# A perceiver's cross-attention: a context block's projection in one piece instead of two

## The chip, the cores and the metric

The kernel runs on one core of a Trainium2 chip. The metric is the device time of one execution in microseconds (us); the time given for a kernel is the median of several runs. One execution was recorded by the hardware profiler, and all rows of the profile come from it. Engines: PE (TensorE: matrix products; PEld is its weight load), DVE (VectorE), ACT (ScalarE), POOL (GpSimd) and SP, which here only issues transfers (DMA).

## The reference

Four layers work on 128 tokens of 256 dims, `x`. Each has a cross-attention over a context of 12544 rows of 192 dims, a self-attention among the 128 tokens, and a mixture of experts. The change is in the cross-attention of layers 0 to 2 (16 heads of 16 dims):

```python
k = (context @ Wk).reshape(B, M, HEADS, hd).transpose(0, 2, 1, 3)
v = (context @ Wv).reshape(B, M, HEADS, hd).transpose(0, 2, 1, 3)
scores = jnp.einsum('bhid,bhjd->bhij', q, k) * scale
scores = jnp.where(context_mask[:, None, None, :], scores, max_neg)
attn = jax.nn.softmax(scores, axis=-1)
out = jnp.einsum('bhij,bhjd->bhid', attn, v)
```

That is layer 0, which alone has a mask. Layers 1 and 2 add biases to the projections, and layer 1 clips the scores and replaces them by a mean where one is not a number (the guard). Layer 3 has another form of attention, with heads of 64 dims.

## The kernel before

All is 32-bit float. The context is cut into 25 blocks of 512 keys (the last has 256). It lies transposed in memory, dims on partitions, and since 192 dims are more than 128 partitions, a block comes as two transfers: `ctxA`, the upper 128 dims of all 512 keys, and `ctxB`, the lower 64 dims, folded so that each half of the block's keys has 64 partitions. Four tiles of each take turns, so SP loads a block as soon as the block four before it has been read (lines 378 to 396).

The 16 heads are done in two halves of 8 (`g` = 0 and 1, line 600), and each half in two passes over the keys, written in `attend_twice_in`. The first pass projects keys and values of all blocks and finds each head's highest score; the second recomputes the scores, lowers them by that maximum, and takes exponentials and the weighted sum. The change is in the first pass.

One projection of a block (`project`, line 152) fills one *pair*, a PSUM tile of two banks with 128 x 2 x 512 numbers: in each bank 256 columns of keys and 256 of values. The dims are summed in two steps. `low=0` multiplies the upper dims: 2 key products of 256 columns and 4 value products of 128, each with all 128 partitions. `low=1` adds the lower dims: as many products with 64 partitions. A 32-bit product runs as two on PE, so the profile counts 12 for either step. After the lower step ACT copies keys and values out of the pair (lines 127 to 136), in layers 1 and 2 with the keys' bias. In layer 1 POOL also adds up the context for the guard (lines 98 and 99), which DVE reduces at lines 931 and 932.

`highest` (line 530) makes scores: a pair again, two products of 32 partitions x 512 keys (line 538; in layer 0 each begins with a product that brings in the mask, line 537, from a row that POOL makes), and one maximum on DVE over 128 x 1024 numbers (line 539, tile `parts`). A block has four of these: two sets of 64 query-and-head combinations (`s` = 0, 1) times two halves of the heads (`half`). That is eight score products a block. The four of one `s` work in four separate groups of 32 rows of the array and run beside each other.

All pairs, for projections and scores alike, come from one pool of four (`self.psum(ppr=4)`, line 501). A new tile takes the buffer that has been free longest in the order of the program, and waits until its last reader is done. PE works in the order in which its products are listed.

What stands between the scores is listed by `steps` (line 138). The first pass has 50 steps, one for each block and `s`; after step `t`'s two maxima come the projections in `steps[t]`. Two blocks are projected before the pass in any case, in layers 1 and 2 eight before its first half (`early`, line 88, beside the layer before). So 23 are left to spread over 46 steps, or 17 in the first halves of layers 1 and 2. The last three blocks get only keys there (`values` is false); their values follow after the pass, while DVE works on the maxima found.

These lines set what is left to do and how fast it is spread:

```python
todo = [(b, low, b < NSB - 3) for b in range(2, NSB) for low in range(2) if g * NSB + b >= self.done]
to = min(n, -(-n * (t + 1) // (2 * NSB - 4)))
while to < n and 2 * todo[to][0] + todo[to][1] <= t + 4:
```

An entry is half a projection, so with 46 entries each step has one: the upper piece after `s` = 0, the lower one after `s` = 1. With 34 entries, two of every three to four steps have one.

Of the kernel before, what the change touches and what calls it, by code (L numbers as in the profile page):

```python
# [28 lines left out]
HB = SB // 2  # L29
NSB = -(-S2 // SB)  # L30
# [14 lines left out]
def bc(ap, axis, n):  # L45

    ap = ap.unsqueeze(axis)
    shape = list(ap.shape)
    shape[axis] = n
    return ap.to_broadcast(shape)  # L50


class Keys:
# [4 lines left out]
    def __init__(self, net, wk, wv, groups, bias=None, sums=None):  # L58
        self.net, self.nc, self.wk, self.wv, self.bias, self.sums = net, net.nc, wk, wv, bias, sums
        self.context = net.context(groups * NSB)  # L60
        self.started, self.done, self.rest = {}, 0, None
        if sums is not None:
            self.nc.gpsimd.memset(sums, 0.0)

# [23 lines left out]
    def early(self, n=EARLY):  # L88

        for b in range(n):  # L90
            for low in range(2):
                self.project(0, b, low)

    def add_up(self, g, b):
        if g == 0 and self.sums is not None:
# [42 lines left out]
    def steps(self, g):  # L138

        todo = [(b, low, b < NSB - 3) for b in range(2, NSB) for low in range(2) if g * NSB + b >= self.done]
        n, at, out = len(todo), 0, []
        for t in range(2 * NSB):
            to = min(n, -(-n * (t + 1) // (2 * NSB - 4)))
            while to < n and 2 * todo[to][0] + todo[to][1] <= t + 4:
                to += 1
            out.append(todo[at:to])
            at = to
        return out  # L150

    def project(self, g, b, low, values=True):


        if g * NSB + b < self.done:
            return
        if not low:
            self.add_up(g, b)
            self.started[g, b] = self.net.early_pair() if self.rest is None else self.net.pair()
        p = self.started[g, b]  # L160
        self.keys_into(p, g, low, [b])
        if values:
            self.values_into(p, g, low, [b], HB)
        if low:
            n = len(self.halves(b))
            self.keep_keys(g, b, p[:, :n, :HB])
            if values:
                self.keep_values(g, b, p[:, :n, HB:])
            self.done = g * NSB + b + 1

    def project_values(self, g, blocks):
        p = self.net.pair()
# [33 lines left out]
class Net:  # L206
# [300 lines left out]
    def attend_twice_in(self, pool, o, qz, keys, masked, clip, between):  # L507
# [11 lines left out]
        def mask_rows(g, b):  # L519

            src = d["mask"].rearrange("c p -> (c p)")[b * SB : min(S2, b * SB + SB)].unsqueeze(0)
            n = src.shape[-1]
            to = rows8[b % 3]
            nc.sync.dma_start(to[0:P:32, :n], src.to_broadcast([4, n]))
            row = pool.tile([P, SB], BF16, tag="row", name="row", bufs=3)
            nc.gpsimd.tensor_scalar(row[:, :n], to[:, :n], 0.0, 1.0, ALU.is_gt, ALU.subtract)
            nc.gpsimd.tensor_scalar(row[:, :n], row[:, :n], self.bar, None, ALU.mult)
            return row

        def highest(g, b, s, half, parts):  # L530

            n = min(SB, S2 - b * SB)
            x = self.pair()
            for i in range(2):
                r = tiles[2 * half + i]
                if masked:
                    nc.tensor.matmul(x[:, i, :n], self.ones16[r, :], rows[-1][r, :n], start=True, stop=False)
                nc.tensor.matmul(x[:, i, :n], qz[r, g, s, :], keys.kT(b)[r, :n], start=not masked, stop=True)  # L538
            nc.vector.tensor_reduce(parts[:, s, 2 * half : 2 * half + 2, b], x[:, :, :n], AX.X, ALU.max)  # L539

        def lowered(parts):


            neg = self.stat(8, "neg8").rearrange("p (s t) -> p s t", s=2)
            nc.vector.tensor_reduce(neg, parts, AX.X, ALU.max, negate=True)
            if clip is not None:
                self.ts(neg, neg, -clip, clip, ALU.max, ALU.min)
            short = self.sp.tile([P, 2, 4], BF16, tag="short", name="short")
            for j in range(2):
                nc.vector.tensor_copy(short, neg)  # L550
                nc.vector.tensor_copy(wide[:, :, :, j], short)
                self.tt(neg, neg, wide[:, :, :, j], ALU.subtract)
            nc.vector.tensor_copy(wide[:, :, :, 2], neg)
            p = self.pair()
            for s in range(2):
                nc.tensor.transpose(p[:, 0, s * P : s * P + P], wide[:, s].rearrange("p t e -> p (t e)"), self.ident)
            m = pool.tile([P, 2, HB], BF16, tag="low", name="low", bufs=1)
            nc.vector.tensor_copy(m, bc(p[:, 0, :HB], 1, 2))  # L558
            return m.rearrange("p c n -> p (c n)")
# [30 lines left out]
        def weighted(g, c, es, acc):  # L590
            v = keys.v(c // 4)
            for j in range(2):
                for s in range(2):
                    for t in range(4):
                        nc.tensor.matmul(  # L595
                            acc[32 * t : 32 * t + 17, s, :P], v[:, c % 4 + j, 2 * t + s, :], es[t // 2][:, t % 2, j, s, :],
                            start=c + j == 0, stop=c + j == S2 // P - 1,
                        )

        for g in range(2):  # L600
            if g == 0:
                for b in range(2):
                    for low in range(2):
                        keys.project(g, b, low)
            parts = pool.tile([P, 2, 4, NSB], F32, tag="parts", name="parts", bufs=1)
            steps = keys.steps(g)
            for b in range(NSB):
                if masked:
                    rows.append(mask_rows(g, b))
                for s in range(2):  # L610
                    for half in range(2):
                        highest(g, b, s, half, parts)
                    for step in steps[2 * b + s]:
                        keys.project(g, *step)
                if between is not None and g == 0 and b == 3:
                    between[0]()

            keys.project_values(g, [NSB - 3, NSB - 2])
            keys.project_values(g, [NSB - 1])
            if between is not None:  # L620
                between[1][g][0](self.pair)
            m = lowered(parts)
            if between is not None:
                between[1][g][1]()
            floor = None
            if clip is not None:
                floor = []
                for half in range(2):
                    x = self.pair()
                    for i in range(2):  # L630
                        r = tiles[2 * half + i]
                        nc.tensor.matmul(x[:, i, :], self.ones16[r, :], m[r, :], start=True, stop=True)
                    floor.append(pool.tile([P, 2, SB], F32, tag=f"floor{half}", name="floor", bufs=1))
                    self.ts(floor[half], x, -clip, None, ALU.add)
            acc = self.pair()
            nc.vector.memset(acc[:, :, :P], 0.0)
            made = []
            for c in range(0, S2 // P, 2):
                made.append((g, c, [weights(g, c, half, m, floor) for half in range(2)], acc))
                if len(made) > (1 if clip is None else 2):  # L640
                    weighted(*made.pop(0))
            if g == 0:
                for b in range(2):
                    for low in range(2):
                        keys.project(1, b, low)
            for step in made:
                weighted(*step)
            oT = pool.tile([P, 2, P], F32, tag="oT", name="oT", bufs=1)
            nc.vector.tensor_copy(oT, acc[:, :, :P])  # L649
            p = self.pair()  # L650
            for s in range(2):
                nc.tensor.transpose(p[:, 0, s * P : s * P + P], oT[:, s, :], self.ident)
            new = p[:, 0, :HB].rearrange("p (s t e) -> p s t e", s=2, t=4)
            r = self.stat(8, "r8").rearrange("p (s t) -> p s t", s=2)
            nc.vector.reciprocal(r.unsqueeze(3), new[:, :, :, 16:17])
            to = o[:, g * P : g * P + P].rearrange("p (t s e) -> p s t e", s=2, e=16)
            for s in range(2):
                self.tt(to[:, s], new[:, s, :, :16], bc(r[:, s], 2, 16), ALU.mult)
# [1082 lines left out]
```

## Time and profile before

| | us |
|---|---|
| median of 4 runs | 3122.86 (3120.72 to 3126.52) |
| the profiled execution | 3123.04 |
| its span, first to last instruction | 3121.2 |
| layer 0, first pass, maxima of both halves | 21.0 to 154.9, 295.2 to 429.9 |
| layer 1, the same | 698.6 to 822.0, 958.8 to 1089.4 |
| layer 2, the same | 1378.6 to 1500.8, 1641.9 to 1772.5 |

The times of the passes are the starts of their first and last maximum. A row of the profile reads: line, engine, operation, output<-inputs, shapes, count, then busy time and mean duration, then the engine's idle time before them and what ended it. In a timeline the first two columns are start and duration of a run of like instructions, and in brackets the idle time before it and its releaser. In the view of one tile, "PE pair L538: 12.0, 11" says that the engine sat idle 12.0 us in 11 stretches until a product of line 538 ended. Times of PE's products overlap, because they are pipelined, so the start of the next group says more than the end of the last.

### The profile page before, as it was taken

Reading aid. Unit: us, or ns where it says so; the run is one execution under the profiler, and the core shown is the slowest. Engines: PE = TensorE matmul, PEld = TensorE weight load, DVE = VectorE, ACT = ScalarE, POOL = GpSimd, SP = SyncE. Lnnn points to the kernel's source line nnn. Section 1 sums busy time; section 2 is a strip of 40 time slices with the busy share of each in tenths; the row PEclk is TensorE's granted clock in tenths of the full one; section 3 lists DMA queues with packets and bytes.
Section 4 is the critical chain, followed back from the end, with each engine's and each line's share of the span. In section 5 each row is a group of like instructions: output and inputs, shape, how many; then the busy total and the mean of one; then the engine's idle time right before and its main releaser. Section 6 shows DMA issues by size and latency. Waiting matters only on the chain.

```text
span 3121.2 us, 78239 instructions
## 1 busy us (share of the span) xinstructions
PE 2971.7 (95%) x35065; PEld 2253.6 (72%) x35065; DVE 1957.4 (63%) x2300; ACT 1470.0 (47%) x1869; POOL 295.3 (9%) x349
## 2 busy tenths in 40 slices
PE   8999999879999999899999999899999999999979
PEld 6677667545576576665676576489889889889858
DVE  7801850439997897769208603467777777777844
ACT  1187139511383185311572285256556555556521
POOL 6601640212000000110000001000000000000000
PEclk9999989989999998999999999899999999999979
DMA  4100210552002102341102105322222222222436
GB/s 134 52 18 26 69 41 3 186 201 60 27 3 62 50 18 70 127 132 51 31 8 72 50 3 198 123 82 84 84 79 88 81 86 81 87 81 85 121 108 204
DMA packets 165254, 246.83 MB, mean 79 GB/s; under 512 B 19853, under 2 KB 106831, under 8 KB 164920
## 3 DMA queue, kind: packets, MB, share of 16 engines
q1 hardware_dynamic: 160200, 227.67, 23.3%
q0 software_dynamic: 4608, 14.16, 1.4%
q8 instruction: 275, 4.51, 0.6%
q14 instruction: 59, 0.48, 0.0%
q10 hardware_dynamic: 112, 0.01, 0.0%
HBM read 241.65 MB, written 0.13 MB: 77 GB/s over the span
## 4 chain that ended last, share of the span: by engine, by line
PE 79%; DVE 11%; ACT 5%; issue 3%; DMA 2%; POOL 0%; SPq 0%; DVEq 0%; ACTq 0%; POOLq 0%
PE pair L102 20%; PE pair L538 9%; PE v L102 8%; PE pair L575 7%; PE pair L595 6%; PE sc L701 6%; PE acc L743 6%; PE ps L275 4%; DVE parts L539 3%; ACT e L581 3%; PE acc L275 2%; PE pair L567 2%; DVE e L289 2%; PE kv L102 2%; PE ps L1532 1%
## 5 line engine op out<-in xcount | busy, mean ns | idle before, releaser
L539 DVE TENSOR_REDUCE parts<-pair 128x2 f32<-128x1024 f32 x600 | 679.3, 1198 | 105.0 <-PE pair L538 104.9
L102 PE MATMUL pair<-ctxA,wk 128*128 128x256 f32 x1236 | 329.0, 399 | 1.4 <-ACT kT L193 1.1
L649 DVE COPY oT<-pair 128x256 f32<-128x256 f32 x6 | 2.5, 425 | 507.8 <-PE pair L595 507.8
L102 PEld LDWEIGHTS pair<-ctxA,wk 128*128 128x128 f32 x1236 | 217.2, 190 | 140.0 <-DVE parts L539 96.0
L538 PE MATMUL pair<-kT,qz 32*128 32x512 f32 (+1 forms) x1632 | 277.8, 615 | 9.7 <-DVE parts L539 9.3
L703 ACT COPY kept<-sc 128x1024 f32<-128x1024 f32 (+1 forms) x135 | 136.2, 1009 | 260.7 <-PE sc L701 260.6
L286 DVE TENSOR_TENSOR top<-top,kept 128x1024 f32<-128x1024 f32 (+2 forms) x145 | 169.1, 1169 | 134.9 <-ACT kept L703 133.7
L575 PE MATMUL pair<-qz,kT 32*128 32x256 f32 x3168 | 251.7, 374 | 0.0
L581 ACT ACTIVATE e<-pair,maskcol 128x512 f32<-128x512 f32 x392 | 237.4, 689 | 20.0 <-PE pair L575 19.1
L289 DVE SCALAR_TENSOR_TENSOR e<-pair,floor 128x1024 f32<-128x1024 f32 x196 | 230.5, 1220 | 7.1 <-PE pair L575 1.1
L587 ACT ACTIVATE e<-e 128x1024 f32<-128x1024 f32 x196 | 207.2, 1057 | 38.2 <-DVE e L289 30.6
L583 ACT ACTIVATE e<-pair 128x1024 f32<-128x1024 f32 x196 | 189.9, 1021 | 60.3 <-PE pair L575 60.3
L595 PE MATMUL pair<-e,v 128*17 128x128 f32 x6336 | 212.3, 274 | 2.0 <-ACT e L587 1.0
L575 PEld LDWEIGHTS pair<-qz,kT 32*128 32x128 f32 x3168 | 205.5, 187 | 10.7
L132 ACT ACTIVATE kT<-pair,bk 128x512 f32<-128x512 f32 (+1 forms) x68 | 45.9, 675 | 348.9 <-PE pair L102 323.6
L595 PEld LDWEIGHTS pair<-e,v 128*17 128x17 f32 x6336 | 156.5, 97 | 67.1 <-issue 42.5
L701 PE MATMUL sc<-qz,kT 64*128 64x128 f32 x2816 | 197.8, 279 | 0.0
L567 PE MATMUL pair<-low,ones 32*128 32x512 bf16 x1176 | 191.7, 391 | 3.6 <-DVE low L558 3.1
L102 PEld LDWEIGHTS v<-wv,ctxA 128*128 128x128 f32 x1568 | 189.8, 192 | 6.4 <-issue 1.9
L102 PE MATMUL v<-wv,ctxA 128*128 128x128 f32 x1568 | 193.1, 276 | 0.0
L102 PE MATMUL pair<-ctxB,wk 64*128 64x256 f32 x1236 | 188.5, 398 | 0.0
L701 PEld LDWEIGHTS sc<-qz,kT 64*128 64x128 f32 x2816 | 171.6, 187 | 13.0 <-issue 1.3
(425 smaller groups left out, 4877.0 us busy)
## 6 DMA issues: line engine op xcount, KB each, us to landing
ctxA<-in_ctxA SPq DMA_DIRECT2D x324, 256.0 KB
ctxB<-in_ctxB SPq DMA_DIRECT2D x339, 128.0 KB
w<-in_L_ffn_W SPq DMA_DIRECT2D x32, 1024.0 KB
ctxA<-in_ctxA POOLq DMA_DIRECT2D x36, 256.0 KB, 3.5
w<-in_L_ffn_w_gateT SPq DMA_DIRECT2D x8, 1024.0 KB
wu<-in_L_ffn_w_upT SPq DMA_DIRECT2D x8, 1024.0 KB
w<-in_L_ffn_w_downT SPq DMA_DIRECT2D x8, 1024.0 KB
w<-in_L_ffn_w1T SPq DMA_DIRECT2D x8, 1024.0 KB
```

What stands on the lines that cost most here:

```text
L102: self.nc.tensor.matmul(out, a, b, start=start and not low, stop=low == 1, skip_group_check=True)
L275: self.nc.tensor.matmul(out, lhsT, rhs, start=(i == 0), stop=(i == n - 1))
L289: self.nc.vector.scalar_tensor_tensor(out, a, s, b, op0, op1, **kw)
L538: nc.tensor.matmul(x[:, i, :n], qz[r, g, s, :], keys.kT(b)[r, :n], start=not masked, stop=True)
L539: nc.vector.tensor_reduce(parts[:, s, 2 * half : 2 * half + 2, b], x[:, :, :n], AX.X, ALU.max)
L567: nc.tensor.matmul(x[:, i, :], self.ones16[r, :], m[r, :], start=True, stop=False, skip_group_check=True)
L575: nc.tensor.matmul(at, kT[r, k], q, start=False, stop=True, skip_group_check=True)
L581: nc.scalar.activation(to[:, :, part], x[:, :, part], AF.Exp, bias=self.mask_col[:, c + j : c + j + 1])
L583: nc.scalar.activation(to, x, AF.Exp)
L587: nc.scalar.activation(to, to, AF.Exp)
L595: nc.tensor.matmul(acc[32 * t : 32 * t + 17, s, :P], v[:, c % 4 + j, 2 * t + s, :], es[t // 2][:, t % 2, j, s, :], start=c + j == 0, stop= ...
L701: nc.tensor.matmul(x[:, t, c : c + P], kT[r, c : c + P], qz[r, g, :], start=True, stop=True)
```

## The change

`project` now does both steps of the dims, upper and then lower, in one call, and an entry of `steps` is a whole block. With 23 blocks left, every second step has one, after `s` = 0: a projection of 24 products, then the four score tiles (eight products) of `s` = 1 and of the next block's `s` = 0. With 17 blocks, a projection comes after every second or third step. The bound by which a block must be ready changes with the form of the entries. The pair for the projection is taken and given back within the call. Number and kind of instructions stay; their order changes on PE, and with it that of some loads on SP, of one block's additions on POOL, and of the guard's two reduces on DVE (after 66 and 67 maxima of the pass instead of 67 and 69).

```diff
-        todo = [(b, low, b < NSB - 3) for b in range(2, NSB) for low in range(2) if g * NSB + b >= self.done]
+        todo = [(b, b < NSB - 3) for b in range(2, NSB) if g * NSB + b >= self.done]
...
-            while to < n and 2 * todo[to][0] + todo[to][1] <= t + 4:
+            while to < n and 2 * todo[to][0] <= t + 3:
...
-    def project(self, g, b, low, values=True):
-
+    def project(self, g, b, values=True):
 
         if g * NSB + b < self.done:
             return
-        if not low:
-            self.add_up(g, b)
-            self.started[g, b] = self.net.early_pair() if self.rest is None else self.net.pair()
-        p = self.started[g, b]
-        self.keys_into(p, g, low, [b])
+        self.add_up(g, b)
+        p = self.net.early_pair() if self.rest is None else self.net.pair()
+        for low in range(2):
+            self.keys_into(p, g, low, [b])
+            if values:
+                self.values_into(p, g, low, [b], HB)
+        n = len(self.halves(b))
+        self.keep_keys(g, b, p[:, :n, :HB])
         if values:
-            self.values_into(p, g, low, [b], HB)
-        if low:
-            n = len(self.halves(b))
-            self.keep_keys(g, b, p[:, :n, :HB])
-            if values:
-                self.keep_values(g, b, p[:, :n, HB:])
-            self.done = g * NSB + b + 1
+            self.keep_values(g, b, p[:, :n, HB:])
+        self.done = g * NSB + b + 1
```

The calls in `early` and `attend_twice_in` lose their loop over `low`; there both steps already stood side by side.

More of the change, by code (lines that the diff above doesn't have):

```diff
@@ L60, in __init__ @@
         self.context = net.context(groups * NSB)
-        self.started, self.done, self.rest = {}, 0, None
+        self.done, self.rest = 0, None
         if sums is not None:
@@ L90, in early @@
         for b in range(n):
-            for low in range(2):
-                self.project(0, b, low)
+            self.project(0, b)
     def add_up(self, g, b):
@@ L602, in attend_twice_in @@
                 for b in range(2):
-                    for low in range(2):
-                        keys.project(g, b, low)
+                    keys.project(g, b)
             parts = pool.tile([P, 2, 4, NSB], F32, tag="parts", name="parts", bufs=1)
@@ L643, in attend_twice_in @@
                 for b in range(2):
-                    for low in range(2):
-                        keys.project(1, b, low)
+                    keys.project(1, b)
             for step in made:
```

## The prediction

> **What bounds the kernel now.** I read the page's summary of engines first, then the costliest groups, then the maximum's tile `parts` in six windows (one for each first pass), then the timeline of single blocks.
>
> ```profile
> PE 2971.7 (95%) x35065; PEld 2253.6 (72%) x35065; DVE 1957.4 (63%) x2300; ACT 1470.0 (47%) x1869; POOL 295.3 (9%) x349
> L539 DVE TENSOR_REDUCE parts<-pair 128x2 f32<-128x1024 f32 x600 | 679.3, 1198 | 105.0 <-PE pair L538 104.9
> ```
>
> PE looks full, but the change touches only the first passes, and there DVE sets the pace: 100 reduces a pass, and nearly all of its idle time is one wait, 104.9 us for a score product. By pass, layer 0 to 2, two each:
>
> ```profile
> L539 DVE TENSOR_REDUCE parts<-pair x100: 682/1218/1228, 21.0 to 154.9; 128x2 f32<-128x1024 f32 x96, 128x2 f32<-128x512 f32 x4
>   PE pair L538: 21.0, 22
> ...
> L539 DVE TENSOR_REDUCE parts<-pair x100: 681/1218/1228, 295.2 to 429.9; 128x2 f32<-128x1024 f32 x96, 128x2 f32<-128x512 f32 x4
>   PE pair L538: 22.4, 23
> ...
> L539 DVE TENSOR_REDUCE parts<-pair x100: 687/1217/1228, 698.6 to 822.0; 128x2 f32<-128x1024 f32 x96, 128x2 f32<-128x512 f32 x4
>   PE pair L538: 12.0, 11
> ...
>   PE pair L538: 18.6, 21
> ...
>   PE pair L538: 12.3, 12
> ...
>   PE pair L538: 18.6, 21
> ```
>
> Layers 1 and 2 wait 12.0 and 12.3 us with the first half of the heads (17 blocks left to project) and 18.6 with the second (23 left). So a first pass lasts as long as its reduces plus the gaps between runs of reduces, and I count gaps. One block of layer 1, second half:
>
> ```profile
> 964.21 1.13 PE L102 MATMUL pair<-ctxA,wk 128*128 128x256 f32 x4
> 965.17 1.05 PE L102 MATMUL pair<-wv,ctxA 128*128 128x128 f32 x8
> 966.16 1.14 PE L538 MATMUL pair<-kv,qz 32*128 32x512 f32 x8
> 967.23 0.70 PE L102 MATMUL pair<-ctxB,wk 64*128 64x256 f32 x4
> 967.33 4.62 DVE L539 TENSOR_REDUCE parts<-pair 128x2 f32<-128x1024 f32 x4 [0.92 <-PE pair L538]
> 967.76 0.61 PE L102 MATMUL pair<-wv,ctxB 64*128 64x128 f32 x8
> 968.30 1.44 PE L538 MATMUL pair<-kv,qz 32*128 32x512 f32 x8
> 968.42 0.69 ACT L132 ACTIVATE kv<-pair,bk 128x512 f32<-128x512 f32 x1 [4.38 <-PE pair L102]
> 969.01 0.58 ACT L136 COPY kv<-pair 128x512 f32<-128x512 f32 x1
> 969.74 0.73 PEld L102 LDWEIGHTS pair<-ctxA,wk 128*128 128x128 f32 x4 [0.83 <-DVE parts L539]
> ```
>
> Read: upper piece 964.21 to 966.16 (1.95), scores, lower piece 967.23 to 968.30 (1.07), scores; period 969.74 - 964.21 = 5.54. DVE runs four reduces in 4.62 (1.13 start to start, the last 1.23) and then waits 0.92. The next upper piece waits for a reduce: the four pair tiles go round in the order in which they come free, and it takes the tile freed three back, so two reduces are still to run when it starts. That gives the gap: 0.05 (release to PE) + 1.95 + 1.17 (score start to reduce, 966.16 to 967.33) - 2 x 1.13 = 0.92, as the row says. The loop is tile, piece, score, reduce, tile; not PE's own work.
>
> **The change, part by part.**
>
> Two edits in `project` and `steps` belong together: lower follows upper at once. Instructions and their counts stay; per engine the lists differ in order only (PE; SP's context loads swap places with mask loads; one pair of POOL adds and the guard's two reduces move).
>
> *1. The projection in one piece.* Two blocks are already projected so, at the turn between halves, and the chain of waits gives their price:
>
> ```profile
> 948.75 6.06 PE pair L102 x48
> ```
>
> 6.06 / 2 = 3.03 a block, which is 1.95 + 1.07: nothing gained or lost in the piece itself.
>
> *2. The steady gap without mask.* Now tiles are taken and freed in the same order: four scores, one projection. The projection takes the tile of four back, the first score after the previous projection, and three reduces remain. Gap = 0.05 + 3.03 + 1.17 - 3 x 1.13 = 0.86, against 0.92; period 5.48 against 5.54. Two other waits stay below it: the fourth score needs the projection's tile, free 0.12 + 0.58 + 0.58 + 0.05 = 1.33 after the piece (the two ACT rows); then 1.07 of product, so 2.40 against the 1.17 + 1.23 + 0.05 = 2.45 of the reduce that the next projection waits for. That margin is 0.05 us.
>
> *3. The steady gap with mask (layer 0).* Its block:
>
> ```profile
> 33.46 0.41 PE L537 MATMUL pair<-row,ones 32*128 32x512 bf16 x4
> 34.77 4.64 DVE L539 TENSOR_REDUCE parts<-pair 128x2 f32<-128x1024 f32 x4 [1.08 <-PE pair L538]
> ```
>
> Mask product to reduce is 1.31. Period now 37.23 - 31.51 = 5.72 (starts of upper pieces). After: 3.03 + 1.31 + 1.23 + 0.05 = 5.62.
>
> *4. The first block of a pass.* Only two reduces are queued when the first whole projection starts: gap 1.07 + 3.03 + 1.17 - (1.17 + 1.13 + 1.23) = 1.74, where an upper piece alone left 1.07 + 1.95 + 1.17 - 3.53 = 0.66. That is +1.08 (layer 0: about +1.06 in the second half; +0.5 in the first, whose first reduce is late anyway).
>
> *5. Blocks 22 to 24*, keys only: 1.69 us in one piece (1.06 + 0.63 now), less than three reduces cover, so no gap. Now these blocks leave some 0.1 (0.3 with mask) twice a pass.
>
> *6. First half of layers 1 and 2.* 17 blocks over 46 half-block steps. In halves, many pieces cost DVE nothing, since two or three steps of reduces lie between:
>
> ```profile
> 716.24 11.47 DVE L539 TENSOR_REDUCE parts<-pair 128x2 f32<-128x1024 f32 x10 [0.85 <-PE pair L538]
> 728.57 1.23 DVE L539 TENSOR_REDUCE parts<-pair 128x2 f32<-128x1024 f32 x1 [0.85 <-PE pair L538]
> ```
>
> Ten reduces run through two pieces here. A whole projection has no such luck: however many steps lie between, it finds three reduces left, because that is what the four tiles allow; so each of the 14 full ones (blocks 8 to 21) costs a gap of 0.86, plus 0.10 for a run that starts anew (1.23 against 1.13). Layer 1 now: gaps 1.92 + 0.92 + 8 x 0.85 = 9.6 in 10 stretches (its 12.0 holds the wait before the first reduce, 2.3). After: 1.74 + 1.26 (1.92 - 0.66: the first upper piece takes 3.25 at 698.54, since the granted clock dips there, mean 0.97 over the pass; that stays) + 13 x 0.86 = 14.2 in 14. Difference 4.6 + 4 x 0.1 - 0.6 (runs now stretched, 3.54 for three reduces at 711.84 against 3.49; some ten of them) = about +4.2, and the same in layer 2.
>
> *7. The guard's reduces* (layer 1, first half) stand after 66 reduces instead of 67 in DVE's queue; behind them stand all later maxima, and PE behind those. They wait for the last context block: 0.63 us now. After, I work it out as load 2.1 + add 0.7 after block 20's upper piece, of which the projection's own gap covers all but 1.2, so about as much in all as now (1.6 with their own 0.69 and 0.41). Ends: -0.6 (the wait of 0.63 goes) to +2 (the load's 2.1 uncovered).
>
> *8. Costed at nothing:* SP's context loads. Four tiles deep, a load has more than two blocks (11 us) of cover for its 2 us; the mask loads that they swap with are ahead by as much. If that cover were gone, 2 us a block.
>
> Sum: layer 0: 19 x -0.105 + 0.5 - 0.6 = -2.0 and 19 x -0.105 + 1.06 - 0.6 = -1.5; second halves of layers 1 and 2: 19 x -0.055 + 1.08 - 0.25 = -0.2 each; first halves +4.2 each. -3.5 - 0.4 + 8.4 = **+4.5 us**. The profiled execution took 3123.04, 0.18 above the median of the four; 3122.86 + 4.5 = **3127.4 us**.
>
> [...]
>
> **Rivals.**
> *Slower by more:* the margin of 0.05 in step 2 is gone, ACT's copies being late. If they free the tile 0.2 later, every full block without mask loses 0.15, 68 x 0.15 = +10: 3138. For: nothing else holds the fourth score; against: ACT is idle 4.38 before each pair of copies. Also here: the guard's upper end, 3129.5.
> *Faster:* the first halves keep DVE fed after all. It decides at one more reduce in store: with four left the gap is 0.05 + 3.03 + 1.17 - 4.52 < 0, so step 6 turns from +4.2 to -9.6 - 1 a pass, and the same in the others; even in the two first halves alone it gives 3122.9 - 3.9 - 21 = 3098. Against: the wait row of the upper piece, which names the reduce, and four tiles.
> *Nothing happens:* the order is changed, but gaps only change places: 3122.9, if step 6's loss is half its size.
>
> **How the numbers follow.** Count of gaps as summed (3124 to 3131): 0.68, of which a fifth lies above 3129.1. Half the loss of step 6 (3120 to 3124): 0.13. Late copies or loads, or the guard at its end (3131 to 3140): 0.14. Gaps filled (below 3116): 0.05. A measurement of this kernel tells about 0.2% (6.2 us) from no change: faster 0.05, same 0.68, slower 0.27. Ends of the range: low, step 6 at +2 each and the steady gains 0.5 better a pass: 3121; high, the guard's 2, a margin lost by 0.05 (68 x 0.05 = 3.4), 1 us of half-rate clock (layer 2 has a 0.64 gap from one): 3134.
>
> **What would show it.** DVE's wait for score products by pass near 20, 21, 17, 18, 16, 18 us (the windows' count, with the wait before the first reduce); one gap of 0.86 for each full projection, also in the first halves of layers 1 and 2; period 5.48 without mask and 5.62 with. Wrong if those first halves keep runs of ten reduces, if a fourth score waits for ACT and the projection after it starts later than the reduce it needs, or if the passes of layer 0 don't shrink.

## The result and the profile after

The kernel after takes 3128.66 us, the median of 41 runs (3121.34 to 3134.60); the kernel before, beside it, takes 3122.10 (61 runs, 3112.13 to 3132.32). The ratio is 1.0019, with a 95% interval of 1.0014 to 1.0024: 5.9 us slower, between 4.4 and 7.5 (the two medians are 6.6 apart). The forecast was 4.5 slower. The prediction also held that a measurement tells only 6.2 us or more from no change, and gave 0.68 to no change that can be told; with so many runs the interval does tell these 5.9 from nothing.

The recorded execution of the kernel after took 3124.77 us (span 3122.7). Lines have moved up by four: line 534 is the score product, 535 its maximum, 101 the projections' products. The page has these totals:

```profile
PE 2975.4 (95%) x35065; PEld 2257.5 (72%) x35065; DVE 1955.7 (63%) x2300; ACT 1469.9 (47%) x1869; POOL 294.6 (9%) x349
...
L535 DVE TENSOR_REDUCE parts<-pair 128x2 f32<-128x1024 f32 x600 | 677.0, 1198 | 111.5 <-PE pair L534 111.5
```

DVE's work is the same to 2 us; its wait for score products has grown from 104.9 to 111.5 us. The maximum's tile, asked for in each first pass by itself, tells where (first halves of layers 0 and 1 in full, then the wait rows of the second half of layer 1 and of both halves of layer 2):

```profile
L535 DVE TENSOR_REDUCE parts<-pair x100: 684/1218/1228, 24.3 to 156.6; 128x2 f32<-128x1024 f32 x96, 128x2 f32<-128x512 f32 x4
...
  PE pair L534: 20.0, 20
...
L535 DVE TENSOR_REDUCE parts<-pair x100: 692/1218/1228, 690.7 to 819.3; 128x2 f32<-128x1024 f32 x96, 128x2 f32<-128x512 f32 x4
...
  PE pair L534: 16.6, 14
...
  PE pair L534: 18.6, 21
...
  PE pair L534: 16.3, 15
...
  PE pair L534: 18.6, 21
```

With 21.4 in the second half of layer 0, the waits by pass are 20.0, 21.4, 16.6, 18.6, 16.3 and 18.6 us, where the prediction named 20, 21, 17, 18, 16 and 18 as its sign. In the first halves of layers 1 and 2, until the last full projection, no more than six maxima stand between two waits, if the guard's counts as one.

From first to last maximum, the six passes take this long (us; read from the starts of single maxima, so with one digit more than the rows above):

| pass | before | after | difference | forecast |
|---|---|---|---|---|
| layer 0, first half | 133.84 | 132.32 | -1.5 | -2.0 |
| layer 0, second half | 134.72 | 133.11 | -1.6 | -1.5 |
| layer 1, first half | 123.42 | 128.59 | +5.2 | +4.2 |
| layer 1, second half | 130.66 | 130.45 | -0.2 | -0.2 |
| layer 2, first half | 122.11 | 125.57 | +3.5 | +4.2 |
| layer 2, second half | 130.66 | 130.45 | -0.2 | -0.2 |
| sum | | | +5.1 | +4.5 |

The two recorded executions as wholes differ by 1.7 only, because work outside the first passes varies from run to run: from the end of layer 0's second maximum pass to layer 1's first maximum the one of before took 268.7 us and the one of after 261.7; in the other ten recorded executions, with halves or whole pieces, it lies between 259.1 and 270.2. So the passes are compared by their own spans, and the kernels by many runs.

Some rows of one block of layer 1, second half, which answers to the one shown of before:

```profile
964.18 2.46 PE L534 MATMUL pair<-kv,qz 32*128 32x512 f32 x16
964.30 0.69 ACT L131 ACTIVATE kv<-pair,bk 128x512 f32<-128x512 f32 x1 [4.32 <-PE pair L101]
...
964.88 0.58 ACT L135 COPY kv<-pair 128x512 f32<-128x512 f32 x1
...
965.36 4.62 DVE L535 TENSOR_REDUCE parts<-pair 128x2 f32<-128x1024 f32 x4 [0.86 <-PE pair L534]
965.51 0.30 PEld L534 LDWEIGHTS pair<-kv,qz 32*128 32x128 f32 x4 [0.18 <-ACT kv L135]
966.64 0.73 PEld L101 LDWEIGHTS pair<-ctxA,wk 128*128 128x128 f32 x4 [0.82 <-DVE parts L535]
...
969.67 2.46 PE L534 MATMUL pair<-kv,qz 32*128 32x512 f32 x16
```

The period is 969.67 - 964.18 = 5.49, the gap 0.86. The fourth score tile starts behind ACT's copy (965.51), the next projection behind a maximum (966.64), both as the prediction had it. The piece is one now, and the gap is nearly what it was.

What the prediction did not have is in layer 1's first half, at the guard. The timeline of DVE:

```profile
771.64 6.88 DVE L535 TENSOR_REDUCE parts<-pair 128x2 f32<-128x1024 f32 x6 [0.86 <-PE pair L534]
780.13 0.69 DVE L925 TENSOR_REDUCE st<-sums 128x1 f32<-128x512 f32 x1 [1.61 <-POOL sums L97]
780.73 1.22 DVE L535 TENSOR_REDUCE parts<-pair 128x2 f32<-128x1024 f32 x1
781.86 0.41 DVE L926 TENSOR_REDUCE st<-sums 128x1 f32<-128x256 f32 x1
782.19 5.74 DVE L535 TENSOR_REDUCE parts<-pair 128x2 f32<-128x1024 f32 x5
```

and that of PE:

```profile
778.21 2.46 PE L534 MATMUL pair<-kT,qz 32*128 32x512 f32 x16
782.00 1.13 PE L534 MATMUL pair<-kT,qz 32*128 32x512 f32 x4 [1.33 <-DVE parts L535]
783.46 1.51 PE L534 MATMUL pair<-kT,qz 32*128 32x512 f32 x4 [0.33 <-DVE parts L535]
784.90 2.07 PE L101 MATMUL pair<-ctxA,wk 128*128 128x256 f32 x4
```

and busy times by stretch (from:to, its length, then PE, PEld, DVE, ACT and POOL busy with their counts, the granted clock, the share of the DMA engines and GB/s):

```profile
778.00:784.10 6.10, 4.44 (x30) 1.68 (x26) 4.49 (x6) 1.17 (x2) 1.45 (x2) 1.00 0.15 43
784.10:787.50 3.40, 3.40 (x12) 2.24 (x9) 3.40 (x4) 0.00 (x0) 0.00 (x0) 0.50 0.00 0
```

The guard's reduce makes DVE wait 1.61, PE runs out of tiles (idle 1.33 and 0.33), and then for 3.4 us it is granted half its clock. The keys' product of 1.13 takes 2.07 (784.90), and the next gap of DVE is 2.43 instead of 0.86. In the kernel before, the same reduce stands one maximum behind the ordinary gap and waits 0.63 (PE idled 1.32 there, as the last row of this document has it, and kept its clock):

```profile
784.42 1.23 DVE L539 TENSOR_REDUCE parts<-pair 128x2 f32<-128x1024 f32 x1 [0.85 <-PE pair L538]
786.28 0.69 DVE L931 TENSOR_REDUCE st<-sums 128x1 f32<-128x512 f32 x1 [0.63 <-POOL sums L98]
```

### The profile page after: what moved, and what is told of

Read it like the earlier page. It is cut to its first block, busy times and chain, and to the rows that moved or that the text cites. A ratio compares the mean times of both kernels' runs of the same rounds, so it can differ in the third digit from the quotient of the medians.

```text
span 3122.7 us, 78239 instructions
## 1 busy us (share of the span) xinstructions
PE 2975.4 (95%) x35065; PEld 2257.5 (72%) x35065; DVE 1955.7 (63%) x2300; ACT 1469.9 (47%) x1869; POOL 294.6 (9%) x349
## 4 chain that ended last, share of the span: by engine, by line
PE 76%; DVE 13%; ACT 5%; issue 3%; DMA 2%; POOL 1%; SPq 0%; DVEq 0%; ACTq 0%; POOLq 0%
PE pair L101 20%; PE v L101 8%; PE pair L534 8%; PE pair L571 7%; PE pair L591 6%; PE sc L695 6%; PE acc L737 6%; DVE parts L535 6%; PE ps L271 4%; ACT e L577 3%; PE pair L563 2%; PE kv L101 2%; DVE e L285 2%; PE acc L271 2%; PE ps L1526 1%
## 5 line engine op out<-in xcount | busy, mean ns | idle before, releaser
L535 DVE TENSOR_REDUCE parts<-pair 128x2 f32<-128x1024 f32 x600 | 677.0, 1198 | 111.5 <-PE pair L534 111.5
L534 PEld LDWEIGHTS pair<-kT,qz 32*128 32x128 f32 x1632 | 108.9, 186 | 119.7 <-DVE parts L535 75.4
```

## The experiments

My theory: DVE's maxima and the gaps between them set the length of a first pass; a gap is set by how many maxima are left when a projection gets its pair tile, two behind a half and three behind a whole. Rivals: PE's own work, or its changes between products of 128, 64 and 32 rows (changes of tiling mode), set the pace; or the loss in layers 1 and 2 is the guard's.

### Whole pieces only where 23 blocks are left

```diff
-        todo = [(b, low, b < NSB - 3) for b in range(2, NSB) for low in range(2) if g * NSB + b >= self.done]
+        left = sum(g * NSB + b >= self.done for b in range(2, NSB))
+        if left == NSB - 2:
+            todo = [(b, (0, 1), b < NSB - 3) for b in range(2, NSB) if g * NSB + b >= self.done]
+        else:
+            todo = [(b, (low,), b < NSB - 3) for b in range(2, NSB) for low in range(2) if g * NSB + b >= self.done]
```

> Whole projections only in the passes with 23 blocks left (both of layer 0, second halves of layers 1 and 2); halves, as before, in the first halves of layers 1 and 2. The theory (gaps of DVE, set by how many maxima are still to run when a projection gets its tile) has the whole loss in those two first halves: without them the change gains 1.5 to 2 in each pass of layer 0 and 0.2 in each second half, 3.5 to 4 us in all, so 3118.3 against 3122.1, ratio 0.9988; gaps of 1.0 (layer 0) and 0.86 once a block. The rival, that the loss has little to do with where the whole projections stand (loads, copies, order elsewhere), has this kernel between the two, at 3124 or more.

Measured: 3115.15 us (12 runs) against 3120.31 (23 runs), ratio 0.9988, 0.9974 to 1.0002. The passes: 132.27, 133.12 in layer 0, 122.98 and 121.32 in the first halves, 130.45 and 130.46 in the second ones. The four passes gain what the change gained in them; against no change at all the interval just does not decide.

### Whole pieces only where 17 blocks are left

The same lines with `left < NSB - 2`.

> The other part alone: whole projections only in the first halves of layers 1 and 2. The theory: +8.7 us by the spans of these passes in the changed kernel's profile (+5.2 and +3.5), so 3130.8, ratio 1.0028, and the spans of all other first passes as before. The rival (the loss is spread, or lies outside the first passes): at most 3128, with other passes longer as well.

Measured: 3124.68 us (13 runs) against the same 3120.31, ratio 1.0016, 1.0006 to 1.0027. The passes say what was expected (layer 0 133.93 and 134.71, layer 1 128.72 and 130.67, layer 2 125.57 and 130.66: +5.3 and +3.5 in the first halves), the sum of 8.8 would be 1.0028, just outside the interval. The loss is in the two first halves, where the trace put it. Its size is settled by the spans better than by the runs' times: the two partial kernels together come to about +1.3 by times, with some 5 us of uncertainty either way (from the two intervals), to +5.2 by the spans of the passes that they change, and the change itself, measured closest, to +5.9.

### Half the maximum's work

```diff
-            nc.vector.tensor_reduce(parts[:, s, 2 * half : 2 * half + 2, b], x[:, :, :n], AX.X, ALU.max)
+            nc.vector.tensor_reduce(parts[:, s, 2 * half : 2 * half + 2, b], x[:, :, : n // 2], AX.X, ALU.max)
```

> The changed kernel with the maximum taken over half of a tile's columns only: it leaves out the other half in the first passes' maxima, which only shift the exponentials. A maximum then takes about 0.69 us instead of 1.22, so DVE and the tile that a projection takes no longer set the period. The theory: the next wait in line is the fourth score's, for the projection's tile, freed by ACT 1.33 after the projection; period without mask 3.03 + 1.33 + 1.07 = 5.43, hardly less than 5.48, and with mask 3.03 + 2.43 = 5.46. The rival, that PE's own work is next: 3.03 + 1.93 = 4.96 without mask. A kernel bound by DVE's work alone would fall by 4 x 0.53 = 2.1 a block.

Measured: 3040.99 us, one run. Rows of two blocks of the timeline:

```profile
959.94 2.48 DVE L535 TENSOR_REDUCE parts<-pair 128x2 f32<-128x512 f32 x4 [2.93 <-PE pair L534]
960.09 0.30 PEld L534 LDWEIGHTS pair<-kv,qz 32*128 32x128 f32 x4 [0.17 <-ACT v L135]
961.15 0.73 PEld L101 LDWEIGHTS pair<-ctxA,wk 128*128 128x128 f32 x4 [0.76 <-DVE parts L535]
...
966.57 0.51 PEld L101 LDWEIGHTS pair<-ctxA,wk 128*128 128x128 f32 x3 [0.76 <-DVE parts L535]
```

The period is 966.57 - 961.15 = 5.42 (5.43 expected), with mask 336.76 - 331.31 = 5.45 (5.46). With maxima of half the length the loop is hardly shorter, since now it runs through ACT's copies and the fourth score tile, the second wait of the prediction's step 2, whose margin in the kernel after was put at 0.05. Halving the step that sets the loop moves the wait and gains 0.07 a block. The kernel is some 80 us faster all the same, since this loop is not everywhere: the passes with 23 blocks are 8 to 9 shorter, those with 17 are 19 to 20. In the latter a projection with six maxima behind it goes from a period of 7.74 to one of 6.60, because there DVE's own time counts in part, and so it does behind the last projection of every pass.

### The kernel after without the guard

```diff
-        sums = self.lw.tile([P, SB + HB], F32, tag="sums", name="sums", bufs=1) if guarded else None
+        sums = None
...
-                    bad, mean = self.nan_guard(own, keys.sums, xT, wq, bq, keys.wk, keys.wv, bk, bv)
-                    nc.vector.copy_predicated(o, bad.bitcast(U32), mean)
```

> The changed kernel without layer 1's guard (it leaves out the sums of the context, their reduces and the replacement of scores that are no numbers). The theory: in layer 1's first half the two long gaps (2.21 and 2.43 in the changed kernel) become 0.86 and none, the half-rate stretch after the first of them goes with it, and the pass is as long as layer 2's, some 125.3 us from first to last maximum instead of 128.6. The rival: the half-rate stretch at 782 has nothing to do with the guard and stays, so the pass keeps a gap of over 2 and lasts 126.5 or more.

Measured: 3113.74 us. The pass took 126.65, which is the rival's number; but where the guard had stood, the timeline has this:

```profile
764.69 4.62 DVE L535 TENSOR_REDUCE parts<-pair 128x2 f32<-128x1024 f32 x4 [0.87 <-PE pair L534]
770.17 6.88 DVE L535 TENSOR_REDUCE parts<-pair 128x2 f32<-128x1024 f32 x6 [0.86 <-PE pair L534]
777.92 6.88 DVE L535 TENSOR_REDUCE parts<-pair 128x2 f32<-128x1024 f32 x6 [0.86 <-PE pair L534]
```

Ordinary gaps, and no stretch at half the clock there. The excess is all in the pass's first gap, 3.61 instead of 2.35, because the half-rate clock that this pass begins with (in both runs) reached further into it, to 3.9 us past the first maximum instead of 1.2. Without that it took 125.4, as expected; the guard then costs the kernel after 128.59 - 125.4 = 3.2.

### The kernel before without the guard

The same lines left out of the kernel before.

> The kernel before without the guard: the sums of the context, the two reduces in the first pass of layer 1 and what follows from them are left out. The changed kernel without it had gaps of 0.86 where the guard's wait and the half-rate stretch had been. Theory (the guard costs the kernel before 1.3 to 1.6 in that pass, and the changed kernel 3.0 to 3.3, because only there the wait lets the granted clock fall): the first half of layer 1 takes 121.8 to 122.3 instead of 123.4, as layer 2's first half does (122.1). Rival (the guard costs as much in both): 120.1 to 120.4. The other five passes as in the kernel before, within 0.3.

Measured: 3109.66 us, the pass 122.22, as expected: 123.42 - 122.22 = 1.2 by the spans. Of the 122.22, 0.42 is a gap late in the pass, beside a stretch at half the clock (807.2 to 810.6) that the kernel before had not, so that the guard itself costs the kernel before 1.6. Behind the guard the clock stayed whole there, as in the two other recorded executions with halves in this pass (the first experiment and the last), where PE idled there for 1.38 and 1.39; with whole pieces and the guard it fell in six executions (at 784.1 in the kernel after, and in other runs at 762.1, 782.4, 786.5, 789.2 and 853.0). The pass as a whole took 122.98 to 123.82 in the three with halves and 128.59 to 129.72 in the five with whole pieces, full maxima and four tiles; most of either spread is the first gap, 1.41 to 2.28 in the three and 2.35 to 3.14 in four of the five, longer where the half-rate clock of the pass's beginning reaches further past the first maximum (1.5 to 3.3 us in the three, 1.2 to 2.8 in the four). What is left of layer 1's loss, 125.4 - 121.8 = 3.6, is step 6 alone, as in layer 2 (3.5).

### One pair tile held, first try

Against the kernel after:

```diff
+            held = self.pair()
+            nc.vector.memset(held[:, :, :1], 0.0)
             for b in range(NSB):
...
+            nc.vector.tensor_copy(self.stat(2, "held"), held[:, :, 0])
             keys.project_values(g, [NSB - 3, NSB - 2])
```

> The changed kernel with one of the four pair tiles held through each first pass, so that three go round (written once before and read once behind it; nothing else differs). Theory (the whole projection takes the tile of four back, three reduces are left): with three tiles it takes the tile of three back, and two reduces are left. Gap 0.05 + 3.03 + 1.17 - 2 x 1.13 = 1.99 instead of 0.86, period without mask 6.61 instead of 5.48, with mask 6.75 instead of 5.62; 68 full blocks without mask and 40 with it give some 115 to 125 us, the kernel about 3250. Rival (PE's own work, or the change of tiling mode, sets the period): 5.48 and 5.62 as they were, the kernel within 10 us of 3128.

Measured: 3123.30 us and the periods of the kernel after. This says nothing for the rival: the closing read stood in DVE's list right behind the memset, since nothing held it back, and the tile was free at once.

```profile
956.28 0.06 DVE L603 MEMSET pair<- 128x2 f32 x1
...
956.38 0.16 DVE L615 COPY st<-pair 128x2 f32<-128x2 f32 x1
```

### One pair tile held, second try

Against the first try:

```diff
-            nc.vector.tensor_copy(self.stat(2, "held"), held[:, :, 0])
+            nc.vector.tensor_tensor(self.stat(2, "held"), held[:, :, 0], parts[:, :, 3, NSB - 1], ALU.add)
```

> The run with a held tile once more, since there the read that was to hold it had been moved to the beginning of the pass and four tiles went round as before (its periods, 5.48 and 5.62, say nothing). Now the read also needs the maxima of the last block, so that the tile is held through the pass. Theory: three tiles, two reduces left: gap 0.05 + 3.03 + 1.17 - 2 x 1.13 = 1.99, period 6.61 without mask and 6.75 with it; the kernel about 115 to 125 us longer. Rival (PE's own work or the change of tiling mode sets the period): 5.48 and 5.62, the kernel within 10 us of 3128.

Measured: 3271.83 us, 143 longer than the kernel after. DVE's timeline in layer 1, second half:

```profile
1049.08 4.62 DVE L535 TENSOR_REDUCE parts<-pair 128x2 f32<-128x1024 f32 x4 [1.99 <-PE pair L534]
1055.69 4.62 DVE L535 TENSOR_REDUCE parts<-pair 128x2 f32<-128x1024 f32 x4 [2.00 <-PE pair L534]
```

Gap 2.00 (1.99 expected), period 6.61; with mask 2.18 and 6.80 (6.75 expected). PE has the same work in the same order, so neither that nor its changes of tiling mode set the period: the number of maxima left does. The 143 are more than my 115 to 125, which counted full blocks only: with three tiles the keys-only blocks leave gaps too (0.66 and 0.84), and in layer 1's first half five gaps grew to between 3.1 and 5.4, in a pass with six stretches at half the clock (the last at its very end).

### Pauses of DVE, first try

The guard's wait was imitated where no guard is, by reduces on DVE that nobody waits for. Against the kernel after:

```diff
+    def pause(self, x, n):
+        self.nc.vector.tensor_reduce(self.stat(1, "pause"), bc(x, 1, n)[:, 0], AX.X, ALU.add)
...
+                if not masked and (clip is None or g == 1) and b in (9, 13):
+                    n = (1000, 1900) if clip is not None else ((1450, 2350), (2800, 3700))[g]
+                    self.pause(parts[:, 1, 3:, b], n[b == 13])
```

> The changed kernel with six reduces more on DVE, which nobody waits for, two in each of three passes without the guard, of 1.2 and 2.15 us (second half of layer 1), 1.67 and 2.62 (first half of layer 2), 3.1 and 4.0 (second half of layer 2), by 0.69 us for 512 elements and 1.22 for 1024. All but the third stand where a projection is already running, so that its gap hides 0.86 of each. Both theories: DVE's own time lengthens the pass by the rest, 0.34 + 1.29, 1.67 + 1.76, 2.23 + 3.18. Theory (a pause of DVE that leaves PE without a tile for about 2 us lets the granted clock fall, as the guard's does): behind the two longest, and perhaps behind those of 1.67 and 1.76, a stretch of some 3.4 us at half the clock follows, and with it a second gap some 1.5 longer: the second half of layer 2 takes 138 to 140 instead of 130.45, the second half of layer 1 132.1. Rival (the fall at 784 in the changed kernel has another cause): no stretch at half the clock in these passes, 132.1, 129.0 and 135.9.

Measured: 3129.40 us; by a slip in the index the reduces read one element each and took 0.15 by their rows (not the 0.06 that the next expectation names), and the passes were within 0.3 of those of the kernel after, but for layer 1's first half (129.58, with a first gap of 3.14). The run says nothing on pauses.

### Pauses of DVE, second try

Against the first try:

```diff
-        self.nc.vector.tensor_reduce(self.stat(1, "pause"), bc(x, 1, n)[:, 0], AX.X, ALU.add)
+        self.nc.vector.tensor_reduce(self.stat(1, "pause"), x.to_broadcast([P, n]), AX.X, ALU.add)
...
-                    self.pause(parts[:, 1, 3:, b], n[b == 13])
+                    self.pause(parts[:, 1, 3, b : b + 1], n[b == 13])
```

> The run with pauses once more: in the last one the six reduces read one element instead of up to 3700 and took 0.06, so that it says nothing on pauses (and one thing on the changed kernel: the stretch at half the clock behind the guard was there again). The places and the lengths are as they were meant: 1.2 and 2.15 (second half of layer 1), 1.67 and 2.62 (first half of layer 2), 3.1 and 4.0 (second half of layer 2). In the traces so far the granted clock comes in pieces of 3.41 us, and the stretch behind the guard follows a piece in which PE was busy for 0.51. Theory (a piece in which PE is idle for more than about 1.6 lets the next run at half the clock): PE's idle stretches are the pauses less the 0.86 that a running projection hides, 0.34 and 1.29, 1.67 and 1.76, 2.23 and 3.18. The first two leave the clock alone, the next two most likely too (they would have to lie in one piece), the last but one makes it fall more likely than not, the last one nearly always; each fall adds a second gap some 1.5 longer. Second half of layer 1: 132.1. First half of layer 2: 129.0, or 130.5. Second half of layer 2: 135.9 and 1.5 to 3 more, 137.4 to 139. Rival (the fall has another cause than PE's idle time): 132.1, 129.0, 135.9, and no stretch at half the clock in them.

Measured: 3143.16 us. Second half of layer 1: 132.03 (132.1 expected). First half of layer 2: 128.73 (129.0). Second half of layer 2: 137.42, where the rival had 135.9. Its DVE timeline around the pause of 3.07 and that of 4.01, and two stretches behind the second:

```profile
1710.81 3.07 DVE L254 TENSOR_REDUCE st<-parts 128x1 f32<-128x2800 f32 x1
1713.80 6.87 DVE L538 TENSOR_REDUCE parts<-pair 128x2 f32<-128x1024 f32 x6
1721.58 4.62 DVE L538 TENSOR_REDUCE parts<-pair 128x2 f32<-128x1024 f32 x4 [0.90 <-PE pair L537]
...
1734.93 4.01 DVE L254 TENSOR_REDUCE st<-parts 128x1 f32<-128x3700 f32 x1
1738.86 6.87 DVE L538 TENSOR_REDUCE parts<-pair 128x2 f32<-128x1024 f32 x6
1748.28 4.62 DVE L538 TENSOR_REDUCE parts<-pair 128x2 f32<-128x1024 f32 x4 [2.55 <-PE pair L537]
```

```profile
1738.00:1741.60 3.60, 1.47 (x8) 0.64 (x12) 3.60 (x4) 0.13 (x1) 0.00 (x0) 1.00 0.12 37
1741.60:1745.00 3.40, 3.40 (x12) 1.63 (x7) 3.40 (x4) 0.00 (x0) 0.00 (x0) 0.50 0.00 0
```

Behind the longest pause PE was busy for 1.47 of 3.60 us, then came one stretch of 3.4 at half the clock, and the second gap was 2.55, 1.65 more than the 0.90 behind the other pause. PE's rows put its idle time at 2.15 there and at 1.22 behind the other; the first two rows are those behind the pauses of 1.66 and 2.60 in layer 2's first half:

```profile
1442.61 1.13 PE L101 MATMUL pair<-ctxA,wk 128*128 128x256 f32 x4 [1.70 <-DVE parts L538]
...
1465.26 1.13 PE L101 MATMUL pair<-ctxA,wk 128*128 128x256 f32 x4 [1.67 <-DVE parts L538]
...
1715.07 2.37 PE L537 MATMUL pair<-kT,qz 32*128 32x512 f32 x12 [1.22 <-DVE parts L538]
...
1740.13 3.16 PE L537 MATMUL pair<-kT,qz 32*128 32x512 f32 x12 [2.15 <-DVE parts L538]
```

The last two are a microsecond less than my 2.23 and 3.18, which were DVE's delays and not PE's. With idle times of 1.70 and 1.67 the clock stayed whole, though PE had idled for no longer than that in all (1.33 + 0.33) when it fell at the guard. One of these six stalls of DVE was followed by half the clock and so paid for twice (4.01 of its own and 1.65 more in the second gap). The other five pauses were paid for once: 1.2 to 3.07 long, less 0.86 where a projection ran beside them.

### A version that is better than both

Layer 0 with whole pieces, first halves of layers 1 and 2 in halves as before, second halves of layers 1 and 2 in two pieces of nearly equal length. The main lines, against the first experiment:

```diff
-        if left == NSB - 2:
+        if left == NSB - 2 and masked:
             todo = [(b, (0, 1), b < NSB - 3) for b in range(2, NSB) if g * NSB + b >= self.done]
         else:
-            todo = [(b, (low,), b < NSB - 3) for b in range(2, NSB) for low in range(2) if g * NSB + b >= self.done]
+            todo = [(b, (low,), b < NSB - 3, left == NSB - 2) for b in range(2, NSB) for low in range(2) if g * NSB + b >= self.done]
...
+            if low and level and values:
+                self.values_into(p, g, 0, [b], HB, only=(1,))
             self.keys_into(p, g, low, [b])
             if values:
-                self.values_into(p, g, low, [b], HB)
+                self.values_into(p, g, low, [b], HB, only=(0,) if level and not low else (0, 1))
```

> A version chosen pass by pass. Layer 0: whole projections as in the change. First halves of layers 1 and 2: halves as before. Second halves of layers 1 and 2: two pieces a block as before, but of about the same length: the first holds the keys' upper product and one column half of the values' upper product (1.51 by their rows), the second the other column half and both lower products (1.72). Theory (the tiles go round in the order in which they come free, and a piece finds two reduces left behind a half and three behind a whole): each gap of the second halves falls by the 0.44 that the longer piece loses, for those pieces that the reduces don't cover; followed tile by tile, the second halves of layers 1 and 2 take 127.5 instead of 130.7, layer 0 132.3 and 133.1 (133.8 and 134.7 before), the first halves stay at 123.0 and 121.5. Sum -1.5 - 1.6 - 3.2 - 3.2 = -9.5, ratio 0.997. Rival (the number of changes of tiling mode sets the time, which is the same in the second halves): these stay at 130.7 or grow, -3 or less, ratio 0.999 or more.

Measured: 3111.50 us (8 runs) against 3120.78 (13 runs), ratio 0.9971, 0.9959 to 0.9983: 9 us faster than the kernel before, between 5.3 and 12.8. The tile `parts` in layer 1's second half, and two pieces of its timeline:

```profile
L544 DVE TENSOR_REDUCE parts<-pair x100: 679/1216/1228, 957.8 to 1085.1; 128x2 f32<-128x1024 f32 x96, 128x2 f32<-128x512 f32 x4
...
  PE pair L543: 13.5, 41
```

```profile
981.83 2.36 DVE L544 TENSOR_REDUCE parts<-pair 128x2 f32<-128x1024 f32 x2 [0.22 <-PE pair L543]
...
984.62 2.35 DVE L544 TENSOR_REDUCE parts<-pair 128x2 f32<-128x1024 f32 x2 [0.43 <-PE pair L543]
```

Both second halves take 127.32 (127.5 expected, 130.66 before); the other passes took 131.94 and 133.12 in layer 0 and 123.82 and 122.06 in the first halves (132.3, 133.1, 123.0 and 121.5 expected). The 0.92 a block has become 0.22 + 0.43, in twice as many gaps. The rival had the number of changes between the forms of product as the same; counted by the rows of the products (128, 64 and 32) it is even one more, five a block instead of four, since the second piece begins with products of 128 rows and goes on with 64. So more changes went with less time.

## Why the prediction was right

The sum held: +4.5 forecast, +5.1 in the six passes of the traces, +5.9 (4.4 to 7.5) in the times. The mechanism was the one forecast; that the sum comes so close is in part luck, since errors of single terms cancel: +1.6 at the guard and +0.6 at the beginning of layer 0 against about 0.6 less in each first half of layers 1 and 2. (As written, the terms of step 6 add up to 4.4 and not 4.2, those of layer 0's first half to -2.1 and not -2.0; the sum would be +4.8.) By its steps:

- *1, 2 and 3, the piece and the steady gaps:* right. 0.86 without mask in all second halves, 1.00 with mask (period 5.62), and the fourth score waits behind ACT's copy, but not long enough to matter. The margin there was worked out from two rows as 0.05; the half-length maxima, where that wait leads, show the period at which it would begin to count, 5.42 against 5.49: 0.07.
- *4, the first block:* 1.74 in the second halves of layers 1 and 2, as worked out, against 0.66. In layer 0's first half it was put too low: from the first maximum to the seventh the pass took 8.01 before and 9.06 after, +1.05 where the terms gave about +0.4.
- *5, keys-only blocks:* no gap is left behind block 21 in any pass.
- *6, the first halves of layers 1 and 2:* right in kind and almost in size. Each of the 13 full projections behind the first has a gap of 0.86 (but for one of 0.92 in layer 1 and the two at the guard), where runs of ten maxima had passed two pieces without any. Layer 2 came to +3.5 instead of +4.2, mostly since a gap of 0.64, from a stretch at half the clock late in that pass of the kernel before (1489.7 to 1493.1), was not there after. In layer 1 the first gap was 2.35 instead of the 3.00 that I had carried over from the kernel before.
- *7, the guard's reduces:* the step whose size was off most. Its direct part was right: with the wait of 1.61 the next maximum came 1.35 late (780.73 against the 779.38 at which it would have come behind an ordinary gap), and the second reduce took 0.33 more, 1.7 in all where I had 1.6. What I left out is what PE does in the meantime. It stood idle for 1.33 + 0.33, the granted clock fell to a half for 3.4 us, and the next gap was 1.57 longer. Together 3.2 against the 1.6 that the guard costs the kernel before. I had a microsecond of half-rate clock in the range, but not at this place and not as a consequence of this wait.
- *8, the loads:* right for the first passes: the maxima wait for score products alone, and the only wait for a load that counts is the guard's own, through POOL, as before.

The number of PE's changes of tiling mode did not set the pace. With a quarter fewer of them, three a block instead of four, the second halves gained 0.2; with a quarter more, but shorter pieces, they gained 3.3. What a single change costs was not shown by any run.

Of the rivals, *faster* is ruled out by the runs of maxima in the first halves, which no longer pass over a projection, and *nothing happens* by the 3.5 and 5.2 that these passes lost; *late copies* (*slower by more*) did not occur, though with maxima of half the length they do.

## What to carry to other kernels

Where producers and consumers share a rotation of tiles, ask for each piece how many consumers are still to run when its tile comes free; the gap is the piece's way to the next consumer less these, and neither engine's busy share tells it. Merging two pieces adds one consumer of cover (1.13 here) and the whole length of the second piece (1.08). Where every block had a gap already, that gains the small difference (0.92 to 0.86 here); where runs of consumers passed over the pieces without a gap, it costs a whole gap (0.86). Making pieces equal paid more here (0.92 to 0.22 + 0.43). A wait placed in the consumer's queue is to be priced with what the producer's clock does afterwards (1.57 more of gap here).

## What the runs showed of the hardware

The fall of TensorE's clock after so short a wait was not expected. In the recorded executions of the kernels before and after, the granted clock was whole or half, and each stretch at half was 3.41 us long or a whole number of times that, up to seven (784.08 to 787.49 and 1220.97 to 1244.87 in the kernel after), but for one that the end of the record cuts off; in the run with long pauses one lay at 1741.6 to 1745.0. Idle for 1.33 and soon after for 0.33 at the guard, or for 2.15 behind the longest pause, PE lost half its clock; idle for 1.22 behind the pause of 3.07, or for 1.32 at the guard of the kernel before (the row below), it kept it. But no limit follows from these rows: idle for 1.70 and 1.67 behind the two pauses in layer 2's first half PE kept its clock too, in the run with half the maximum's work it lost half of it at 762.1, after the guard had left it idle for 0.85, and in the run with three tiles it did so at 781.3, where PE's rows show no idle time above 0.19 in the eleven microseconds before. A row's idle time counts from the modelled end of the product before, and how much the place of the wait within such a stretch decides was not tried. That the fall follows the guard's stall with whole pieces is shown (in six executions, and not without the guard); what makes the clock fall in general, and how long a stall it takes, stays open.

```profile
788.15 1.24 PE L538 MATMUL pair<-kT,qz 32*128 32x512 f32 x8 [1.32 <-DVE parts L539]
```
